# Layer 2 weights as 16-bit exponents with three bf16 parts of the support, in place of the Gelu pair factor of layer 3

## The chip, the cores and the metric

The kernel runs on one core of a Trainium2 chip. The metric is device time in microseconds. Engines are called as in the profile: PE is TensorE, PEld its weight load, DVE VectorE, ACT ScalarE, POOL GpSimd and SP SyncE.

## What is computed

Four graph layers work on N = 3327 nodes with D = 64 features and one sparse weighted adjacency matrix of N x N. Each layer normalises x, cuts it at zero and adds the layer's output to x. Layers 0 (two gated convolutions) and 1 (hyperbolic) are the same in both kernels. The change concerns layers 2 and 3, which are in the reference:

```python
def _L2_gnn_ref(input, adj, weight, bias):
    support = input @ weight
    mask = (adj != 0).astype(support.dtype)
    rank = jnp.cumsum(mask, axis=1)
    deg = rank[:, -1:]
    k = jnp.minimum(deg, float(MAX_NEIGH))
    pos = rank - (deg - k)
    w = mask * jnp.where(pos > 0, DECAY ** (k - pos), 0.0)
    out = w @ support + bias
    return out
...
x_tan = _logmap0(x, C)
left = x_tan @ att_W[:D] + att_b
right = x_tan @ att_W[D:]
adj_att = jax.nn.sigmoid(left + right.T) * adj
x_local = _logmap(x[:, None, :], x[None, :, :], C)
support_t = jnp.einsum('ij,ijd->id', adj_att, x_local)
return _proj(_expmap(x, support_t, C), C)
```

So in layer 2 the weight of a neighbour is a half to the power of the number of neighbours behind it in the row, for at most 100 of them. In layer 3 every pair of nodes has a factor that comes from its hyperbolic distance, and a sigmoid attention, and what is summed over neighbours is that factor, times the attention, times the neighbour's features.

## The kernel before, in words

The nodes are padded to 3328, which makes 26 blocks of 128 (`NB`, `P`). The adjacency comes transposed: one block holds 128 neighbours j on the partitions and all nodes i in the free dimension, 1664 KB. An aggregation keeps the output transposed in four accumulators of PSUM (`acc`); the lower half of their partitions holds the features for the first 1664 nodes (`HN`), the upper half for the others, each in four chunks of 416 (`NQ`, `CH`). The helper of line 241 issues each such matmul; its stationary operand has 64 columns. Four of the 26 adjacency blocks stay resident in SBUF, the rest are streamed anew for each aggregation through three buffers (`adj_block`, L157).

Layer 2 (L349 to L423) goes through the blocks backwards. For each block VectorE makes a 0/1 mask in bf16 (L379). For each of the eight chunks TensorE counts, for each node i, the neighbours behind this one: one matmul with a triangular matrix over the block's mask (L384), which also subtracts 1024 where the mask is set, and one with ones over the sum of the masks of later blocks (`behind`, L392). ScalarE turns the count into the bits of a power of two, as int32 read as f32 (L400). VectorE multiplies it with a test that the count is small enough (L402), and the f32 product `w` goes into the accumulating matmul (L241), two chunks later (`flush(2)`). VectorE adds the mask to `behind` (L416). Here a scheduler chooses the order of instructions on each engine; counts have four banks of PSUM (`scratch`).

Layer 3 is written in an order by hand (`manual_schedule`, L442). The preparation (L487 to L619) packs three bf16 parts of per-node values into rows that DMAs carry into `rows_i`, `rows_j` and `rows_l` (L588, L594). The loop (L743 on) has 26 steps `n`: two output halves times 13 pairs of neighbour blocks. For each, `pair_values` takes one product of 64 features per pair of nodes in f32 (L635) plus a bf16 matmul of the packed rows (L646); ScalarE applies Gelu to the sum (L654), Tanh for the attention (L661), and in two of three steps a Square (L669). VectorE multiplies the attention with the adjacency (L675), in the third of the steps does the square (L680), and multiplies both factors (L687). `gather` sums over neighbours (L703 for the features, L714 for a scalar). A flag `within` (L619) tells whether all squared norms lie in the range for which the fit with Gelu was made. If not, a general version (L763 to L931) recomputes layer 3; on these inputs the branch skips it.

This general version matters below. Its functions are `distances` (L830: per chunk two f32 matmuls, a max with a small number, a second max, then their product), `root_ln` and `root_exp` (L849, L852: ScalarE), `norms` (L855: two VectorE passes), `attention` (L862: Sigmoid, and a product with the adjacency on GpSimd), `logs` (L868: two Ln on ScalarE, a subtraction on GpSimd), `gather` (L875: two products on VectorE, then four matmuls). They work on tiles of 128 x 1664 f32, in groups of two neighbour blocks (`G1 = 2`), in this order:

```python
run(distances, 0)
for g in range(len(groups) + 1):
    ...
    run(root_ln, g)
    run(root_exp, g)
    run(attention, g)
    run(gather, g - 1)
    run(norms, g)
    run(distances, g + 1)
    run(logs, g)
```

The tail (L936 to L982) turns the sums into the output by passes of 128 x 1664 on VectorE.

Of the kernel before, what the change touches and what calls it, by code (L numbers as in the profile page):

```python
# [33 lines left out]
EXP_UNIT = 2.0**23  # L34


X2_LEAST = 22.0
HA = 2.5897813538797263
HB0 = 2.28574309955982
HG = -7.090763495839726  # L40
HK = 0.012618748686465375
HD = 0.7055609776434136 / HK

# [12 lines left out]
def gnn_kernel(ctx: ExitStack, tc: tile.TileContext, t, out):  # L56
# [80 lines left out]
    with ExitStack() as c012:  # L137
# [4 lines left out]
        ps = c012.enter_context(tc.tile_pool(name="ps", bufs=4, space=PSUM))  # L142

        def scratch(name):
            return ps.tile([P, 512], F32, name=name, tag="ps")
# [202 lines left out]

        with ExitStack() as c2:  # L349
# [12 lines left out]
            V.memset(ebias, (127.0 - MASK_ON) * EXP_UNIT)  # L362
# [3 lines left out]
            linear(h_t, w_l2, m_n)  # L366

            acc = accumulators()
            behind = None
            pending = []  # L370

            def flush(keep):
                while len(pending) > keep:
                    accumulate(acc, *pending.pop(0))

            for j in reversed(range(NB)):
                a = adj_block(j)
                mask = mk.tile([P, NP], BF16, name="mask", tag="mask")
                V.tensor_scalar(mask, a, 0.0, None, op0=OP.not_equal)  # L379
                for h in range(2):  # L380
                    for q in range(NQ):
                        i0 = h * HN + q * CH
                        p = scratch("cnt")
                        T.matmul(  # L384
                            p[:, :CH],
                            lhsT=tri,
                            rhs=mask[:, i0 : i0 + CH],
                            start=True,
                            stop=behind is None,
                        )  # L390
                        if behind is not None:
                            T.matmul(  # L392
                                p[:, :CH],
                                lhsT=ones,
                                rhs=behind[:, i0 : i0 + CH],
                                start=False,
                                stop=True,
                            )
                        bits = wk.tile([P, CH], I32, name="bits", tag="bits")
                        S.activation(bits, p[:, :CH], AF.Relu, bias=ebias, scale=-EXP_UNIT)  # L400
                        w = wk.tile([P, CH], F32, name="w", tag="w")
                        V.scalar_tensor_tensor(  # L402
                            w,
                            p[:, :CH],
                            MAX_NEIGH - MASK_ON,
                            bits.bitcast(F32),
                            op0=OP.is_lt,
                            op1=OP.mult,
                        )
                        pending.append((q, h, m_n[:, slot(j), :], w, j == NB - 1, j == 0))  # L410
                        flush(2)
                if behind is None:
                    behind = mask
                elif j:
                    nxt = mk.tile([P, NP], BF16, name="behind", tag="behind")
                    V.tensor_add(nxt, behind, mask)  # L416
                    behind = nxt
            flush(0)
# [14 lines left out]

    c3 = ctx.enter_context(ExitStack())  # L440
    n3 = c3.enter_context(tc.tile_pool(name="n3", bufs=1))
    c3.enter_context(tc.manual_schedule())  # L442

    attw = n3.tile([P, 2, D], F32, name="attw")
    attb = n3.tile([P, 1], F32, name="attb")
    aw, ab = t["att_W"], t["att_b"]
    nc.sync.dma_start(attw, bass.AP(tensor=aw.tensor, offset=aw.offset, ap=[[0, P], [D, 2], [1, D]]))
    nc.sync.dma_start(attb, bass.AP(tensor=ab.tensor, offset=ab.offset, ap=[[0, P], [1, 1]]))
    h = n3.tile([P, NB, D], F32, name="h3")
    sums = n3.tile([P, NB, D + 1], F32, name="sums")  # L450

    with ExitStack() as cf:
        f3 = cf.enter_context(tc.tile_pool(name="f3", bufs=1))
        wk = cf.enter_context(tc.tile_pool(name="wkf", bufs=2))
        ps_acc = cf.enter_context(tc.tile_pool(name="ps_accf", bufs=1, space=PSUM))
        ps = cf.enter_context(tc.tile_pool(name="psf", bufs=1, space=PSUM))

        def pair_tile(i):
            return ps.tile([P, 2, 512], F32, name="pt", tag=("pta", "ptb")[i % 2])


        pairs = [(hf, c) for hf in range(2) for c in range(HB)]
        adj2 = t["adjT"].rearrange("(h c p) n -> c p h n", h=2, p=P)
        adjs = {}

        def load3(n):
            if n < len(pairs):
                hf, c = pairs[n]
                adjs[n] = a = wk.tile([P, 2, HN], F32, name="adj3", tag="adj3")
                nc.sync.dma_start(a, adj2[c][:, :, hf * HN : (hf + 1) * HN])  # L470

        load3(0)
        load3(1)


        rows_j = f3.tile([P, NP], BF16, name="rows_j")
        rows_i = f3.tile([P, NP], BF16, name="rows_i")
        G.memset(rows_j, 0.0)
        G.memset(rows_i, 0.0)
        identb = f3.tile([P, P], BF16, name="identb")  # L480
        V.tensor_copy(identb, ident)
        ones3 = f3.tile([3, P], BF16, name="ones3")
        V.memset(ones3, 1.0)
        hg = f3.tile([P, 1], F32, name="hg")
        V.memset(hg, HG)

        layernorm_relu(n3, h)  # L487

        last = f3.tile([P, 1], I32, name="last")
        G.iota(last, pattern=[[0, 1]], base=0, channel_multiplier=1)  # L490
        lastf = f3.tile([P, 1], F32, name="lastf")
        V.tensor_scalar(lastf, last, P - 1.0, None, op0=OP.is_equal)
        kb = slot(NB - 1)
        V.tensor_scalar(h[:, kb, :], h[:, kb, :], lastf, None, op0=OP.max)
        x2 = sumsq(n3, h, "x2")


        q = small(n3, "q")
        V.tensor_scalar(q, x2, 0.5, -0.5, op0=OP.mult, op1=OP.add)
        V.reciprocal(q, q)  # L500
        xd = f3.tile([P, HB, 3, D], F32, name="xd")
        qv = q.rearrange("p (c a) -> p c a", a=2)
        V.tensor_mul(
            xd[:, :, :2, :],
            h.rearrange("p (c a) d -> p c a d", a=2),
            qv[:, :, :, None].to_broadcast([P, HB, 2, D]),
        )
        G.tensor_copy(xd[:, :, 2, :], xd[:, :, 0, :])

        xs = f3.tile([P, HN], F32, name="xs")  # L510
        xw = f3.tile([P, HN], F32, name="xw")
        for n, (dst, a) in enumerate(((xs, 0), (xw, 1))):
            for c0 in range(0, HB, 8):
                m = min(8, HB - c0)
                p = pair_tile(n + c0 // 8).rearrange("p a b -> p (a b)")
                for c in range(m):
                    T.transpose(
                        p[:, c * P : (c + 1) * P],
                        xd[:, c0 + c, a : a + 2, :].rearrange("p a d -> p (a d)"),
                        ident,  # L520
                    )
                if n:
                    S.activation(dst[:, c0 * P : (c0 + m) * P], p[:, : m * P], AF.Copy)
                else:
                    V.tensor_copy(dst[:, c0 * P : (c0 + m) * P], p[:, : m * P])

        par = f3.tile([P, 4, NB], F32, name="par")
        V.tensor_copy(par[:, 0, :], q)  # L530
        V.tensor_scalar(par[:, 1, :], q, -1.0, -1.0, op0=OP.mult, op1=OP.add)
        V.tensor_scalar(par[:, 2, :], q, -1.0, -HB0 / HA, op0=OP.mult, op1=OP.add)
        pn = small(n3, "pn")
        S.activation(pn, x2, AF.Sqrt)
        V.tensor_scalar(pn, pn, MIN_NORM, None, op0=OP.max)
        kt = artanh(n3, pn, "kt")
        rpn = recip(n3, pn, "rpn")
        V.tensor_mul(kt, kt, rpn)
        sides = []
        for s in range(2):  # L540
            pr = n3.tile([P, NB, D], F32, name="sq", tag="sq")
            V.tensor_mul(pr, h, attw[:, s : s + 1, :].to_broadcast([P, NB, D]))
            r = small(n3, f"side{s}")
            V.tensor_reduce(r, pr, axis=AX.X, op=OP.add)
            V.tensor_mul(r, r, kt)
            sides.append(r)
# [6 lines left out]
        for i in range(3):  # L553
            b = f3.tile([P, 4, NB], BF16, name=f"part{i}")
            V.tensor_copy(b, par)
            if i < 2:
                V.tensor_sub(par, par, b)
# [470 lines left out]
```

## Time and profile before

| | us |
|---|---|
| median of 3 runs | 1162.76 (1161.22 to 1165.96) |
| the profiled execution | 1162.76 |
| its span, from the first to the last instruction | 1160.9 |
| layers 0 and 1 | about 0 to 420 |
| layer 2: preparation, loop | to 470, to 755 |
| layer 3: preparation, loop, tail | to 815, to 1108, to 1161 |

A line of the profile for a group of instructions names the source line, engine, operation, output and inputs by their names in the program, the shape and the count; then follow busy time and the mean duration of one in ns. On the time line the first column is the start and the second the duration, both in us; "x4" means four instructions merged. The time by stretch gives for each stretch its length, then busy us and count of PE, PEld, DVE, ACT and POOL, the clock granted to TensorE, the DMA engines' share and GB/s. The chain of waits follows the last instruction back to what released it. A matmul of f32 shows as two records.

### The profile page before, as it was taken

The page shows a single profiled execution, that of the slowest core. Times are in us where ns is not written, and L with a number is a line of the kernel's source. Part 1 is how long each engine was busy: PE and PEld are TensorE (multiplying, and loading weights), DVE is VectorE, ACT ScalarE, POOL GpSimd, SP SyncE. Part 2 cuts the span into 40 slices and gives each one's busy share as a digit, 9 for nine tenths or more (in the row PEclk, how much of TensorE's full clock was granted, in tenths as well). Part 3 has the DMA queues.
Part 4 walks back from the last instruction along what each step waited for, and adds up shares of the span by engine and source line. Part 5 has one row for each costly group of instructions (what it writes and reads, how often), then busy time and mean ns, then how long its engine had stood idle before and what let it go on. Part 6 is the DMA issues. An engine that isn't in the chain of part 4 may idle for free. (4 is left out here: it accounts for less than half of the span.)

```text
span 1160.9 us, 9585 instructions
## 1 busy us (share of the span) xinstructions
PE 891.9 (77%) x3835; PEld 341.3 (29%) x3835; DVE 638.2 (55%) x716; ACT 386.2 (33%) x452; POOL 9.5 (1%) x18
## 2 busy tenths in 40 slices
PE   2999999997399950999999999911789887889700
PEld 2433453344143320322222222210333333333200
DVE  4000140006800058677777777686588887888778
ACT  1000010002200011444444444400778776787710
POOL 0000000000000000000000000020000000000000
PEclk9999999999599985999999999965899998999955
DMA  8799909993069990143443400020244453444100
GB/s 310 292 385 382 379 5 361 389 396 148 0 255 381 379 385 11 59 176 127 168 164 131 177 1 0 1 120 9 104 147 164 177 177 118 172 145 157 58 3 29
DMA packets 25011, 204.31 MB, mean 176 GB/s; under 512 B 6141, under 2 KB 6269, under 8 KB 13181
## 3 DMA queue, kind: packets, MB, share of 16 engines
q1 hardware_dynamic: 21382, 202.96, 46.0%
q10 hardware_dynamic: 3575, 0.64, 0.3%
q8 instruction: 32, 0.52, 0.2%
q14 instruction: 22, 0.18, 0.0%
HBM read 202.48 MB, written 0.85 MB: 175 GB/s over the span
## 5 line engine op out<-in xcount | busy, mean ns | idle before, releaser
L241 PE MATMUL acc<-adj,m_n 128*64 128x416 f32 x1056 | 271.4, 518 | 15.1 <-DMA adj<-in_adjT 14.7
L241 PE MATMUL acc<-w,m_n 128*64 128x416 f32 x416 | 184.0, 534 | 18.7 <-DVE w L402 18.7
L400 ACT ACTIVATE bits<-cnt,ebias 128x416 int32<-128x416 f32 x208 | 123.2, 606 | 167.2 <-PE cnt L392 156.1
L257 DVE COPY m_t<-acc 128x416 f32<-128x416 f32 x12 | 6.2, 582 | 308.7 <-PE acc L241 308.7
L241 PEld LDWEIGHTS acc<-adj,m_n 128*64 128x64 f32 x1056 | 112.5, 136 | 170.6 <-issue 130.1
L402 DVE SCALAR_TENSOR_TENSOR w<-cnt,bits 128x416 f32<-128x416 f32 x208 | 115.6, 586 | 50.9 <-ACT bits L400 50.7
L675 DVE SCALAR_TENSOR_TENSOR th<-th,adj 128x1664 f32<-128x1664 f32 x52 | 97.5, 1888 | 46.4 <-ACT th L661 46.4
L635 PE MATMUL pt<-xs 64*128 64x416 f32 x208 | 99.2, 558 | 15.4 <-ACT gl L654 15.4
L635 PE MATMUL pt<-xw,xs 64*128 64x416 f32 x208 | 98.8, 556 | 12.3 <-ACT gl L654 12.3
L654 ACT ACTIVATE gl<-pt 128x832 f32<-128x832 f32 x104 | 84.2, 861 | 66.5 <-PE pt L646 66.5
L687 DVE SCALAR_TENSOR_TENSOR gl<-gl,th 128x1664 f32<-128x1664 f32 x52 | 96.0, 1888 | 12.4 <-ACT gl L669 12.1
L703 PE MATMUL accx<-gl,xd 128*64 128x416 f32 x416 | 81.8, 530 | 8.1 <-DVE gl L687 8.1
L280 ACT ACTIVATE gate<-gate,brz 128x416 f32<-128x416 f32 x16 | 9.7, 606 | 234.0 <-PE gate L278 233.9
L661 ACT ACTIVATE th<-leftb,righth 128x1664 f32<-128x1664 f32 x52 | 87.5, 1683 | 0.0
L384 PE MATMUL cnt<-mask,tri 128*128 128x416 bf16 x208 | 71.7, 347 | 1.2 <-DVE mask L379 1.0
L241 PEld LDWEIGHTS acc<-w,m_n 128*64 128x64 f32 x416 | 42.0, 135 | 93.5 <-DVE w L402 46.4
L392 PE MATMUL cnt<-behind,ones 128*128 128x416 bf16 x192 | 65.3, 340 | 0.0
L241 PE MATMUL acc<-res,m_n 128*64 128x416 f32 x192 | 44.0, 545 | 22.2 <-DVE m_n L317 22.2
L416 DVE TENSOR_TENSOR behind<-behind,mask 128x3328 bf16<-128x3328 bf16 x23 | 43.5, 1892 | 30.1 <-PE cnt L392 30.1
L669 ACT ACTIVATE gl<-gl,hg 128x3328 f32<-128x3328 f32 x18 | 55.2, 3069 | 0.0
L197 PE MATMUL tr<-ident,h_n 128*128 128x128 f32 x26 | 5.9, 420 | 63.7 <-DVE h_n L134 63.7
L384 PEld LDWEIGHTS <-tri 128*128 128x128 bf16 x208 | 19.9, 96 | 104.0 <-issue 102.1
(221 smaller groups left out, 713.1 us busy)
## 6 DMA issues: line engine op xcount, KB each, us to landing
adj<-in_adjT SPq DMA_DIRECT2D x114, 1664.0 KB
res<-in_adjT SPq DMA_DIRECT2D x4, 1664.0 KB
xn<-in_x SPq DMA_DIRECT2D x1, 832.0 KB
out<-u SPq DMA_DIRECT2D x1, 832.0 KB
ih<-in_wihT ACTq DMA_DIRECT2D x4, 48.0 KB
hh<-in_whhT ACTq DMA_DIRECT2D x4, 48.0 KB
w<-in_W ACTq DMA_DIRECT2D x4, 16.0 KB
attw<-in_att_W SPq DMA_DIRECT2D x1, 64.0 KB
```

Source lines behind the costliest of these rows:

```text
L241: T.matmul(acc[q][h * D : (h + 1) * D, :CH], lhsT=lhsT, rhs=rhs, start=first, stop=last)
L384: T.matmul(p[:, :CH], lhsT=tri, rhs=mask[:, i0 : i0 + CH], start=True, stop=behind is None,)
L392: T.matmul(p[:, :CH], lhsT=ones, rhs=behind[:, i0 : i0 + CH], start=False, stop=True,)
L400: S.activation(bits, p[:, :CH], AF.Relu, bias=ebias, scale=-EXP_UNIT)
L402: V.scalar_tensor_tensor(w, p[:, :CH], MAX_NEIGH - MASK_ON, bits.bitcast(F32), op0=OP.is_lt, op1=OP.mult,)
L635: T.matmul(pts[b][:, i, :CH], lhsT=xs[rs, c * P : (c + 1) * P], rhs=rhs[rs, q0 : q0 + CH], start=True, stop=False,)
L654: S.activation(gl[:, b, 2 * k * CH : (2 * k + 2) * CH].rearrange("p (i n) -> p i n", i=2), pts[b][:, :, :CH], AF.Gelu, scale=-HA,)
L661: S.activation(th[:, k, :], leftb[:, hf * HN : (hf + 1) * HN], AF.Tanh, bias=righth[:, kk : kk + 1], scale=0.5,)
L669: S.activation(gl, gl, AF.Square, bias=hg)
L675: V.scalar_tensor_tensor(th[:, b, :], th[:, b, :], 1.0, a[:, b, :], op0=OP.add, op1=OP.mult)
L687: V.scalar_tensor_tensor(gl[:, b, :], gl[:, b, :], hd, th[:, b, :], op0=OP.add, op1=OP.mult)
L703: T.matmul(acc[i // 2][(i % 2) * D : (i % 2 + 1) * D, :CH], lhsT=xd[:, c, b, :], rhs=gl[:, b, i * CH : (i + 1) * CH], start=first, stop=last,)
```

## The change

In layer 2 the weights become 16-bit numbers: ScalarE writes the count's power of two straight as the upper 16 bits of a float (`U16`, unit 2**7 instead of 2**23), with a bias that makes counts past the limit zero by the Relu, and the tile is read as bf16. The product on VectorE (L402 of before) is gone. The support, scaled by 2**27, is split into three bf16 parts whose sum is exact, and the accumulating matmuls run once per part in bf16. Counts are in tiles of two banks, two chunks per conversion; the two halves h alternate innermost; the loop is ordered by hand.

In layer 3 the version with Gelu, its preparation, its flag and the branch are gone, and the general version runs always. Its functions are those of before, with small changes ahead of and behind the loop.

```diff
-EXP_UNIT = 2.0**23
+EXP_UNIT = 2.0**7
+U16 = mybir.dt.uint16
...
-            V.memset(ebias, (127.0 - MASK_ON) * EXP_UNIT)
+            V.memset(ebias, (MAX_NEIGH - MASK_ON) * EXP_UNIT)
...
             linear(h_t, w_l2, m_n)
-
+            V.tensor_scalar(m_n, m_n, 2.0**27, None, op0=OP.mult)
+            parts = []
+            for i in range(3):
+                p = mk.tile([P, NB, D], BF16, name=f"part{i}", bufs=1)
+                V.tensor_copy(p, m_n)
+                if i < 2:
+                    V.tensor_sub(m_n, m_n, p)
+                parts.append(p)
...
+            with tc.tile_pool(name="psc", bufs=2, space=PSUM) as psc, tc.manual_schedule():
...
+                def flush(keep):
+                    while len(pending) > keep:
+                        j, k, ws = pending.pop(0)
+                        for i in range(2):
+                            for n, p in enumerate(parts):
+                                for h in range(2):
+                                    accumulate(
+                                        acc,
+                                        2 * k + i,
+                                        h,
+                                        p[:, slot(j), :],
+                                        ws[h][:, i, :].bitcast(BF16),
+                                        j == NB - 1 and n == 0,
+                                        j == 0 and n == 2,
+                                    )
...
+                    V.tensor_scalar(mask, a, 0.0, None, op0=OP.not_equal)
+                    for k in range(NQ // 2):
+                        ws = []
+                        for h in range(2):
+                            p = psc.tile([P, 2, 512], F32, name="cnt", tag="cnt")
+                            for i in range(2):
...
+                            w = wk.tile([P, 2, CH], U16, name="w", tag=f"w{h}")
+                            S.activation(
+                                w, p[:, :, :CH], AF.Relu, bias=ebias, scale=-EXP_UNIT
                             )
-                        bits = wk.tile([P, CH], I32, name="bits", tag="bits")
-                        S.activation(bits, p[:, :CH], AF.Relu, bias=ebias, scale=-EXP_UNIT)
-                        w = wk.tile([P, CH], F32, name="w", tag="w")
-                        V.scalar_tensor_tensor(
-                            w,
-                            p[:, :CH],
-                            MAX_NEIGH - MASK_ON,
-                            bits.bitcast(F32),
-                            op0=OP.is_lt,
-                            op1=OP.mult,
-                        )
-                        pending.append((q, h, m_n[:, slot(j), :], w, j == NB - 1, j == 0))
-                        flush(2)
+                            ws.append(w)
+                        pending.append((j, k, ws))
+                        flush(1)
...
-        for n in range(-1, len(pairs)):
-            if n >= 0:
-                products(n)
-            if n + 1 < len(pairs):
-                pair_values(n + 1)
-                weights(n + 1)
-                load3(n + 3)
...
-        ok = nc.values_load(within, min_val=0, max_val=1)
...
-    with ExitStack() as cg:
-        cg.enter_context(tc.If(ok < 1))
```

The functions of the loop that now runs always, with the line numbers that they have after the change in the first column:

```python
559  p = scratch3(0)
560  T.matmul(p[:, :CH], lhsT=lhsT, rhs=auge[:, cs], start=True, stop=True)
561  V.tensor_scalar(e[:, cs], p[:, :CH], MIN_NORM, None, op0=OP.max)
562  p = scratch3(1)
563  T.matmul(p[:, :CH], lhsT=lhsT, rhs=augd[:, cs], start=True, stop=True)
565  V.scalar_tensor_tensor(d[:, cs], e[:, cs], 2e-7, p[:, :CH], op0=OP.mult, op1=OP.max)
568  V.tensor_mul(e, e, d)
572  S.activation(den[j], den[j], AF.Ln, scale=LN_SCALE)
575  S.activation(den[j], den[j], AF.Exp, scale=-0.5)
579  V.scalar_tensor_tensor(dist[j], dist[j], LN_SCALE**0.5, den[j], op0=OP.mult, op1=OP.mult)
582  V.tensor_scalar(dist[j], dist[j], ONE_LESS, None, op0=OP.min)
587  S.activation(s, leftb, AF.Sigmoid, bias=right[:, k : k + 1])
588  G.tensor_mul(s, s, adjs.pop((hf, j)))
593  S.activation(l, dist[j], AF.Ln, bias=one)
594  S.activation(dist[j], dist[j], AF.Ln, bias=one, scale=-1.0)
595  G.tensor_sub(l, l, dist[j])
599  V.tensor_mul(l, l, den.pop(j))
600  V.tensor_mul(l, l, sig.pop(j))
```

## The prediction

> **What bounds the kernel now.** I read the busy shares first, then the busy time by stretch, and then the time line of one piece of each stretch that the change touches. The stretches are layers 0 and 1 (to 420 us), the preparation of layer 2 (to 470), its loop (to 755), the preparation of layer 3 (to 815), its loop (two stretches, to 1108) and the tail.
>
> ```profile
> span 1160.9 us, 9585 instructions
> ...
> PE 891.9 (77%) x3835; PEld 341.3 (29%) x3835; DVE 638.2 (55%) x716; ACT 386.2 (33%) x452; POOL 9.5 (1%) x18
> ```
> ```profile
> 470.00:755.00 285.00, 264.95 (x833) 68.47 (x833) 201.59 (x261) 122.29 (x207) 0.15 (x1) 1.00 0.28 102
> 755.00:815.00 60.00, 11.35 (x48) 6.64 (x50) 42.43 (x92) 5.04 (x8) 6.57 (x4) 0.59 0.16 62
> 815.00:965.00 150.00, 128.46 (x759) 50.90 (x756) 116.88 (x63) 120.61 (x98) 0.00 (x0) 0.98 0.44 153
> 965.00:1108.00 143.00, 121.86 (x724) 46.93 (x722) 110.89 (x63) 103.46 (x85) 0.00 (x0) 0.97 0.35 127
> ```
>
> The columns are PE, PEld, DVE, ACT and POOL busy, then clock, DMA share and GB/s. In layer 2's loop TensorE is busy 265 of 285 us and the DMA only 28%: TensorE bounds it. In layer 3's loop (293 us) TensorE, VectorE and ScalarE are all at 72 to 86%, and GpSimd is idle. One chunk of layer 2's loop, and one gather of layer 3's, on TensorE:
>
> ```profile
> 504.91 0.35 PE L384 MATMUL cnt<-mask,tri 128*128 128x416 bf16 x1
> 505.10 0.34 PE L392 MATMUL cnt<-behind,ones 128*128 128x416 bf16 x1
> 505.37 0.91 PE L241 MATMUL acc<-w,m_n 128*64 128x416 f32 x2
> 506.21 0.35 PE L384 MATMUL cnt<-mask,tri 128*128 128x416 bf16 x1
> ```
> ```profile
> 904.16 3.01 PE L703 MATMUL accx<-gl,xd 128*64 128x416 f32 x16
> ```
>
> A chunk takes 1.30 us from start to start. A bf16 matmul of 416 columns streams in about 0.175; an f32 one is two records of 0.35 each (416 records for 208 calls). Those sum to 1.05; the other 0.25 goes at the two changes between 128- and 64-column use. In the gather neighbours write alternate halves of the accumulator: 16 records of 0.35 take 3.0 us, so two run side by side.
>
> **What the Trainium skill says.** "TensorE: Matmul & The Clock Gate", Part 3, says that matmuls on different column groups run concurrently; the gather line agrees (0.175 per record instead of 0.35), and layer 2 now does not use it. Its Part 1 says that an idle array falls to half its clock. The trace agrees: layer 3's first f32 passes, after an idle spell, start 0.70 apart (814.21, then 814.90 on the time line), later 0.35. "ScalarE: Activation LUTs", What ACT_TABLE_LOAD costs, gives about 1283 ns per load; the loads in this trace take 1283 ns. "SBUF — State Buffer", Who interferes with whom, says that GpSimd and a VectorE operation that uses two ports, or has two SBUF inputs while GpSimd reads, lock each other out for a whole instruction. For two-port operations the trace agrees:
>
> ```profile
> 757.66 2.95 POOL L479 MEMSET rows_i<- 128x3328 bf16 x1
> ```
> ```profile
> 758.03 2.61 DVE L127 TENSOR_SCALAR ln_mean<-ln_mean 128x26 f32<-128x26 f32 x1
> ```
>
> This small operation takes 0.18 elsewhere and here ends with the memset. For two SBUF inputs no row of before has GpSimd beside it.
>
> **The change, part by part. Layer 2.** It removes 208 f32 products (L402, 586 ns) from VectorE and 416 f32 passes from TensorE. ScalarE has 104 conversions of 832 columns instead of 208 of 416; L654, of that shape, takes 861 ns. For each half block of source nodes (52 of them) TensorE gets 8 count matmuls (8 x 0.175 = 1.40) and 12 bf16 matmuls with neighbours in opposite halves (6 pairs x 0.175 = 1.05), plus one double change of use, 0.25: 2.70 us. Beside it lie ScalarE with 1.7 us, VectorE with 1.9 (mask and running sum, L379 and L416, 3.77 per block), and the DMA with 2.2 per half block at the 390 GB/s of layer 0. The count tile is free in time: its conversion ends some 1 us before TensorE comes back to it, so ordering by hand costs nothing while TensorE is latest; if ScalarE were late by more than that, each half block would grow by the excess.
>
> New ahead of the loop are a scaling and three casts (about 1.0 each, from L379's 1883 ns for twice the elements) and two subtractions (1.9 each): 7.8 us on VectorE, on the path, since the first products need all three parts. They end at 469.6 + 7.8 = 477.4. Two half blocks of counts are done by then, so the end comes at 477.4 + 52 x 2.70 - 1.4 = 616. Now the last product ends at 753. Saved: 137 us, and layer 3 starts at 756 - 137 = 619.
>
> **Layer 3.** Its loop becomes the one that before holds as a fallback (line 763 on) and doesn't run here, so it has to be costed from rows of like shape. Preparation on VectorE, all on the path: normalising 11.2, squared norm 3.9, artanh chain 5.2, three products and two reductions of 1664 elements 9.6, transposed copies (0.85 per 512 columns, as at L202) with their fills 22: 52 us, so it ends at 671. The seven transfers of packed rows (L588, L594) and ScalarE's 21 us of waiting for them go with the old preparation. The loads on SyncE's queue become half as large (0.85 MB) and twice as many; each waits for GpSimd to free one of three buffers, but is wanted a round later, so it is hidden.
>
> A round handles two blocks of neighbours. VectorE: gather, four two-input passes of 1664 elements at 1.9 = 7.65; norms, two of 1.9 and two one-input passes of 1.0 = 5.9; distances, 16 operations of 416 columns from PSUM (0.58 and 0.59 in dependent pairs, 8.9) and two products of 1.9 = 12.7. TensorE needs 16 x 0.70 for the distances and starts them cold after its idle stretch, which I put at 1.3 us. Sum 27.3 us. ScalarE: ten passes of 1.68 and, by the instruction order of the built kernel, three table loads of 1.28: 20.6, and the Exp that the norms need ends 6.3 us into the round, under the gather. GpSimd: four two-input passes. The GPSIMD page's 4497 ns for 2048 elements (GPSIMD Engine Reference, Elementwise) gives an estimate of 3.65 each, 14.6. So VectorE bounds the round: 27.3 without any clash of ports.
>
> The clash is the unknown. Least: none, 27.3. Most: every two-input and two-port pass takes turns with GpSimd: mul after the first norm (9.55 to 13.2), then each following norm pass waits for one GpSimd pass, and the first distance product for the end of the last: 3.65 x 3 + 1.5, a round of 39.9. I take the middle: VectorE's next pass follows 0.02 us after the last one (the chain of waits shows such steps), so I let it keep the port through gather and norms. GpSimd's passes then run during the PSUM operations; each distance product waits for the second of two: 13.55 + 7.3 + 1.9 = 22.75, + 4.45, sub passes to 30.05, + 1.9 = 31.95. If only two-port passes clash, the same count gives 32.4.
>
> A half is: first distances 14, a first round without gather 28.9, eleven rounds of 31.95 = 351.5, and at the end norms, GpSimd's four passes, the last gather and the collection of sums 40.8. That is 435; two of them, with 14 us of transposed copies between, 884. The tail from the last sums now takes 52.4, less 3.9 of waiting at the branch that goes: 48.5. Span: 671 + 884 + 48.5 = 1603.5. The run of the profile was 1162.8 us for a span of 1160.9, and is itself the median of the three; with these 1.9 us: **1605**.
>
> **Rivals.** Taking turns (39.9 per round): a half is 14 + 29.4 + 438 + 44 = 525, so 1786. The skill's sentence on two SBUF inputs speaks for it; against it, the trace never shows GpSimd getting in between two VectorE passes. No clash (27.3): a half is 375, so 1487; against it stands the blocked L127. Layer 2's pairs don't overlap, because each bf16 pass needs its own weight load (135 ns for an f32 one now): 12 x 0.175, or 55 us more, 1660. The other side: not slower needs a round of about 12.5 us (2 x 11 x 12.5, with the other pieces in proportion, fills 1161 - 671 - 48.5 - 14). That could come only if VectorE's f32 two-input passes ran at two elements a cycle; 1.0 us for a one-input pass speaks for such a rate, 1.88 for every two-input row against it, and ScalarE's 20.6 would hold the round anyway. That the change doesn't do what it says, with the fallback already running in before, is excluded: no such line is in its trace.
>
> **Numbers.** Forecast 0.43 (its own range 1570 to 1650); taking turns 0.30; no clash 0.15; pairs apart 0.08; the other side 0.02; the rest, 0.02, lies above. The range reaches over the rivals' times, 1480 to 1800. A measurement of this kernel can tell about 0.5% from no change. Faster 0.02, same 0.01, slower 0.97.
>
> **What would show it.** Layer 2: matmuls of L240 in pairs, 5.4 us per block, a loop of about 140 us with ScalarE at some 60%. Layer 3: 26 rounds, VectorE nearly always busy, ScalarE near 65%, three table loads a round; the duration of L579, L582 and L568 says which clash: 1.9, 1.0 and 1.9 for none, 4 to 6 us where they wait for GpSimd. I am wrong if GpSimd's passes are far from 3.65 us, or if rounds end on ScalarE or TensorE.

## The result, and the profile after

| | us | ratio to before |
|---|---|---|
| before | 1162.28 (beside it) | 1 |
| after, median of 4 runs | 1859.16 (1857.56 to 1864.29) | 1.599, 95% from 1.595 to 1.604 |
| forecast | 1605 (1480 to 1800) | |

The change makes the kernel 697 us slower. The sign was foreseen; the time lies 254 us above the forecast and 59 us above the range. The profiled execution has a span of 1856.7 us. The head of its page, with busy times and the clock granted to TensorE (tenths of full speed, in 40 slices of the span):

```profile
span 1856.7 us, 10430 instructions
...
PE 1231.3 (66%) x3897; PEld 561.0 (30%) x3897; DVE 1245.1 (67%) x1067; ACT 657.1 (35%) x509; POOL 421.2 (23%) x118
...
PEclk9999997995999676556655666675666665566565
```

TensorE is busy for 339 us more than before with only 62 more matmul records, and from the 14th slice on (603 us) its clock is at 0.5 to 0.7 throughout, against 0.97 in layer 3 of before. A matmul takes longer there, so a good part of the added "busy" is the clock and not work. The busy time by stretch (length, then PE, PEld, DVE, ACT, POOL, clock, DMA share, GB/s) puts the time in its place:

```profile
470.00:619.00 149.00, 142.12 (x1039) 68.34 (x1038) 97.39 (x60) 91.80 (x102) 0.00 (x0) 0.98 0.54 199
...
700.00:1232.00 532.00, 334.84 (x587) 145.43 (x586) 437.76 (x311) 243.04 (x160) 196.57 (x49) 0.60 0.12 39
```

Layer 2's loop ends at 615.4 us (forecast 616) with TensorE busy for 95% of it and the clock at 0.98. The stretch from 700 to 1232 us, nearly all of the first half of layer 3's loop, has no engine near its limit: TensorE 63%, VectorE 82% (waits inside its passes included, as shown below), and the clock at 0.60. One half block of layer 2 on TensorE's time line (starts and durations in us):

```profile
540.62 1.25 PE L240 MATMUL acc<-w,part 128*64 128x416 bf16 x12
541.80 0.35 PE L409 MATMUL cnt<-mask,tri 128*128 128x416 bf16 x1
...
543.04 0.34 PE L417 MATMUL cnt<-behind,ones 128*128 128x416 bf16 x1
543.31 1.25 PE L240 MATMUL acc<-w,part 128*64 128x416 bf16 x12
```

From 540.62 to 543.31 is 2.69 us, where the forecast had 2.70. So the search is for layer 3 alone. One round of it on VectorE, from the end of the gather to the first distance:

```profile
1022.61 1.89 DVE L600 TENSOR_TENSOR lnp<-lnp,sig 128x1664 f32<-128x1664 f32 x1
1024.42 1.88 DVE L579 SCALAR_TENSOR_TENSOR dist<-dist,den 128x1664 f32<-128x1664 f32 x1
1026.34 4.42 DVE L582 TENSOR_SCALAR dist<-dist 128x1664 f32<-128x1664 f32 x1
1030.68 5.38 DVE L579 SCALAR_TENSOR_TENSOR dist<-dist,den 128x1664 f32<-128x1664 f32 x1
1036.10 4.39 DVE L582 TENSOR_SCALAR dist<-dist 128x1664 f32<-128x1664 f32 x1
1040.41 0.58 DVE L561 TENSOR_SCALAR den<-pd 128x416 f32<-128x416 f32 x1
```

GpSimd beside it ("x2" is two passes back to back):

```profile
1026.12 8.19 POOL L588 TENSOR_TENSOR sig<-sig,adj 128x1664 f32<-128x1664 f32 x2 [21.92 <-ACT sig L587]
1035.60 4.00 POOL L595 TENSOR_TENSOR lnp<-lnp,dist 128x1664 f32<-128x1664 f32 x1 [1.29 <-ACT dist L594]
1044.06 3.70 POOL L595 TENSOR_TENSOR lnp<-lnp,dist 128x1664 f32<-128x1664 f32 x1 [4.45 <-ACT dist L594]
```

Read the two by their ends. The first L579 is free, 1.88. At 1026.12 GpSimd begins, and the L582 that VectorE issues at 1026.34 lasts until 1030.76, though it needs 1.03. Then L579 (needs 1.88) ends at 1036.06, after GpSimd's second pass (1034.31). The third GpSimd pass is issued at 1035.60 and ends at 1039.60; the last L582 (needs 1.03) ends 0.9 us after it, at 1040.49. VectorE issues its next pass within 0.05 us of the last one, and still a GpSimd pass lies between each two. The lengthened durations are waits; no idle time is shown.

And TensorE in the same round:

```profile
1020.83 7.43 PE L603 MATMUL ac<-lnp,hn 128*65 128x416 f32 x16 [6.33 <-DVE lnp L600]
1028.10 0.86 PE L560 MATMUL pd<-auge,augj 66*128 66x416 f32 x2
...
1030.19 0.86 PE L563 MATMUL pd<-augd,augj 66*128 66x416 f32 x2
1041.04 1.75 PE L560 MATMUL pd<-auge,augj 66*128 66x416 f32 x2 [9.98 <-DVE den L561]
1042.59 1.59 PE L563 MATMUL pd<-augd,augj 66*128 66x416 f32 x2
...
1056.45 1.59 PE L563 MATMUL pd<-augd,augj 66*128 66x416 f32 x2
```

After the gather it runs four distance matmuls ahead, 0.70 us apart, until the four tiles of PSUM for distances are full. Then it idles 9.98 us, while VectorE is in the norms, and the other twelve come 1.39 us apart: half speed, for 17 us, and it never recovers within them. They end the round: in its last block VectorE waits 0.80 us for each.

The round is 43.55 us on VectorE (L599 at 1016.96 and 1060.52): gather 7.46, norms 15.99, distances 20.10.

### The profile page after: what moved, and what is told of

Its sections match the earlier page's. It is cut to its first block, busy times and chain, and to the rows that moved or that the text cites. A ratio compares the mean times of both kernels' runs of the same rounds, so it can differ in the third digit from the quotient of the medians.

```text
span 1856.7 us, 10430 instructions
## 1 busy us (share of the span) xinstructions
PE 1231.3 (66%) x3897; PEld 561.0 (30%) x3897; DVE 1245.1 (67%) x1067; ACT 657.1 (35%) x509; POOL 421.2 (23%) x118
## 4 chain that ended last, share of the span: by engine, by line
PE 30%; issue 26%; DVE 24%; POOL 11%; DMA 8%; ACT 1%; ACTq 0%; POOLq 0%; DVEq 0%
PE acc L240 13%; DMA adj<-in_adjT 7%; POOL lnp L595 6%; POOL sig L588 5%; PE pd L560 5%; PE pd L563 5%; DVE dist L582 5%; DVE dist L579 4%; PE cnt L409 2%; DVE lnp L600 2%; DVE lnp L599 2%; PE cnt L417 2%; DVE den L568 1%; DVE sq L74 1%; PE ac L603 1%
## 5 line engine op out<-in xcount | busy, mean ns | idle before, releaser
L560 PE MATMUL pd<-auge,augj 66*128 66x416 f32 x416 | 289.0, 791 | 235.3 <-DVE den L561 235.2
L588 POOL TENSOR_TENSOR sig<-sig,adj 128x1664 f32<-128x1664 f32 x52 | 212.9, 4114 | 958.2 <-ACT sig L587 958.2
L603 PE MATMUL ac<-lnp,hn 128*65 128x416 f32 x416 | 210.7, 675 | 188.4 <-DVE lnp L600 182.0
L563 PE MATMUL pd<-augd,augj 66*128 66x416 f32 x416 | 284.6, 781 | 0.0
L595 POOL TENSOR_TENSOR lnp<-lnp,dist 128x1664 f32<-128x1664 f32 x52 | 205.6, 3956 | 135.2 <-ACT dist L594 135.2
L572 ACT ACTIVATE den<-den 128x1664 f32<-128x1664 f32 x52 | 82.7, 1590 | 423.7 <-DVE den L568 387.1
L582 DVE TENSOR_SCALAR dist<-dist 128x1664 f32<-128x1664 f32 x52 | 222.3, 4275 | 1.8
L565 DVE SCALAR_TENSOR_TENSOR dist<-den,pd 128x416 f32<-128x416 f32 x208 | 122.3, 588 | 104.6 <-PE pd L563 95.4
L579 DVE SCALAR_TENSOR_TENSOR dist<-dist,den 128x1664 f32<-128x1664 f32 x52 | 182.0, 3500 | 9.1 <-ACT den L575 9.1
L561 DVE TENSOR_SCALAR den<-pd 128x416 f32<-128x416 f32 x208 | 122.1, 587 | 68.8 <-PE pd L560 68.4
L563 PEld LDWEIGHTS pd<-augd,augj 66*128 66x128 f32 x416 | 121.0, 291 | 123.3 <-issue 103.2
L599 DVE TENSOR_TENSOR lnp<-lnp,den 128x1664 f32<-128x1664 f32 x52 | 98.0, 1884 | 7.2 <-POOL lnp L595 7.2
L568 DVE TENSOR_TENSOR den<-den,dist 128x1664 f32<-128x1664 f32 x52 | 98.4, 1891 | 1.8
```

Source lines behind the costliest of these rows:

```text
L560: T.matmul(p[:, :CH], lhsT=lhsT, rhs=auge[:, cs], start=True, stop=True)
L561: V.tensor_scalar(e[:, cs], p[:, :CH], MIN_NORM, None, op0=OP.max)
L563: T.matmul(p[:, :CH], lhsT=lhsT, rhs=augd[:, cs], start=True, stop=True)
L565: V.scalar_tensor_tensor(d[:, cs], e[:, cs], 2e-7, p[:, :CH], op0=OP.mult, op1=OP.max)
L579: V.scalar_tensor_tensor(dist[j], dist[j], LN_SCALE**0.5, den[j], op0=OP.mult, op1=OP.mult)
L582: V.tensor_scalar(dist[j], dist[j], ONE_LESS, None, op0=OP.min)
```

## The experiments

The theory after the result: two things add up. (a) VectorE and GpSimd take turns at each pass; this lengthens the norms by some 10 us. (b) TensorE idles meanwhile, and distance matmuls with 66 rows do not get the clock back. Rivals: (a) alone, with a clock that doesn't matter; (b) alone, with matmuls of 66 rows slow whatever comes before; and layer 2 having a part in it. A round is the distance between the first norm passes of neighbouring rounds, the same for all full rounds of a kernel within the spread given. "One run" is a single execution without an interval. Line numbers differ a little between the kernels.

| kernel | us | full round, us |
|---|---|---|
| after | 1859.2 | 43.5 to 43.6 |
| 128 rows | 1757.9, one run | 39.1 to 39.5 |
| GpSimd's passes on VectorE | 1652.9, one run | 34.0 to 35.8 |
| the same, 128 rows | 1638.1, one run | 34.0 to 35.8 |
| attention late | 1628.5, one run | 32.1 to 33.7 |
| attention late, 128 rows | 1631.4, one run | 32.1 to 33.3 |
| GpSimd's passes left out | 1475.2, one run | 26.6 to 28.5 |

**Layer 2 alone** ("l2only" in what follows). Layer 2 of after with layer 3 of before, the version with Gelu. Against after, only layer 3 is exchanged; the cut shows its first lines:

```diff
-    with ExitStack() as c3:
-        n3 = c3.enter_context(tc.tile_pool(name="n3", bufs=1))
...
+    c3 = ctx.enter_context(ExitStack())
+    n3 = c3.enter_context(tc.tile_pool(name="n3", bufs=1))
...
```

> The new layer 2 with layer 3 left as before (Gelu version). Theory: layer 2's part of the change did what was forecast, a half block of 2.69 us on TensorE instead of four chunks of 1.37, and all of the loss lies in layer 3. Then 1162 - 137 = 1025 us, with layer 3 as long as before. Rival: part of layer 2's gain is only there because layer 3's general version follows it (its loads or its preparation); then over 1040.

Measured: 1028.72 us (1027.24 to 1030.97, 5 runs), ratio 0.885 (0.883 to 0.887). Layer 2's part gains 134 us (1162.3 - 1028.7; forecast 137), and needs no general layer 3 behind it, so the rival falls. What the exchange of layer 3 then adds is 1859.2 - 1028.7 = 830.5 us.

**Layer 2, the two halves h outermost.**

```diff
-                        for i in range(2):
-                            for n, p in enumerate(parts):
-                                for h in range(2):
+                        for h in range(2):
+                            for i in range(2):
+                                for n, p in enumerate(parts):
```

> As l2only, but the twelve accumulating matmuls of a half block run with the half h outermost, so that six neighbours in a row write the same columns of the array. Theory: pairs in opposite column halves stream side by side and halve this step; without them 52 x 6 x 0.175 = 55 us more, about 1080. Rival: the array overlaps them in any order, or ScalarE hides the step: within 10 us of l2only.

Measured: 1050.0 us, one run: 21 us more, between the two. TensorE's time line:

```profile
540.36 1.62 PE L246 MATMUL acc<-w,part 128*64 128x416 bf16 x12
...
543.42 1.62 PE L246 MATMUL acc<-w,part 128*64 128x416 bf16 x12
```

The half block is 3.06 us instead of 2.69. Alternating the halves is worth 0.37 us per twelve products, and the twelve take 1.55 us (the next count starts at 541.91), less than 0.175 each. So the direction was right and the size wrong: the expectation, like the rival of the prediction in which pairs don't overlap, priced it at 55 us. Why six in a row on the same half cost so little is not shown.

**Layer 2, order left to the scheduler.**

```diff
-            with tc.tile_pool(name="psc", bufs=2, space=PSUM) as psc, tc.manual_schedule():
+            with tc.tile_pool(name="psc", bufs=2, space=PSUM) as psc:
```

> As l2only, but the order of layer 2's loop is left to the scheduler; the instruction order shows counts and products of single parts mixed, with two to six products between counts. Theory: more changes between 128- and 64-column use (0.25 us a pair of changes) and fewer opposite neighbours, 20 to 80 us slower than l2only. Rival: the order by hand is worth nothing, within 5 us.

Measured: 1019.6 us, one run; both expectations missed it on the wrong side. The same kernel, run several times:

> Layer 2 as changed but ordered by the scheduler, layer 3 as before, timed in rounds. Theory from its one look: products of the first part start before the other two parts are made, so the loop ends 9 us earlier than by hand: 1019 us, 0.877 of before. Rival: the one look was chance, 1028 us as with the order by hand.

Measured: 1024.35 us (1020.90 to 1027.35, 5 runs), ratio 0.880 (0.878 to 0.883); layer 2 by hand had 0.885 (0.883 to 0.887). The intervals just meet, so these 4 us are likely and not proven by the times. The time lies between the two expectations. The traces show where a gain would come from. TensorE of the version by hand, at the start of the loop:

```profile
469.25 0.37 PE L246 MATMUL acc<-w,part 128*64 128x416 bf16 x2
471.52 0.56 PE L246 MATMUL acc<-w,part 128*64 128x416 bf16 x2 [1.90 <-DVE part L378]
474.51 1.60 PE L246 MATMUL acc<-w,part 128*64 128x416 bf16 x8 [2.43 <-DVE part L378]
```

The written order puts products with all three parts ahead of the next counts, so TensorE waits for VectorE to cast parts 2 and 3. The scheduler uses part 1 and further counts meanwhile. From the start of the first product to that of the last it is 145.1 us by hand (469.2 to 614.4) and 138.2 in both profiles of the scheduled version; the half block is 2.69 us in all. These 7 us are hard to see in the total because the loop itself began at 467.4 us in one of these profiles and at 473.9 in the other. Of the kernels run, this one has the lowest median.

**128 rows.** The operands of the distance products get 62 more rows of zeros (`auge` like `augd`); the results stay the same.

```diff
-        augj = n3.tile([D + 2, NP], F32, name="augj")
+        augj = n3.tile([P, NP], F32, name="augj")
+        G.memset(augj[D:, :], 0.0)
...
-            augd = n3.tile([D + 2, HN], F32, name="augd", tag="augd")
+            augd = n3.tile([P, HN], F32, name="augd", tag="augd")
+            G.memset(augd[D:, :], 0.0)
```

> The changed kernel with the operands of layer 3's distance matmuls padded with zeros from 66 to 128 rows; the result is the same. Theory: after each idle stretch of 10 us the clock stays at half through all 16 matmuls because only 66 of 128 rows are in use; with all rows it recovers as it does for layer 3's matmuls of before, the pitch falls from 1.39 to 0.70 us within a few us, a round loses 5 to 6.5 us and the kernel ends at 1690 to 1730 us. Rival: the number of rows has no part in it, the idle stretch alone keeps the clock low: 1859 us, granted clock of the loop still 0.60.

Measured: 1757.9 us, one run, 101 us less; the theory's range ended 28 us lower, and a round loses 4.4 us instead of 5 to 6.5. The distances after the idle stretch:

```profile
1009.68 1.75 PE L563 MATMUL pd<-auge,augj 128*128 128x416 f32 x2 [8.92 <-DVE den L564]
...
1014.00 1.57 PE L566 MATMUL pd<-augd,augj 128*128 128x416 f32 x2
1015.38 0.88 PE L563 MATMUL pd<-auge,augj 128*128 128x416 f32 x2
1016.10 0.86 PE L566 MATMUL pd<-augd,augj 128*128 128x416 f32 x2
```

Four matmuls come at the slow pace, then the steps fall to 0.70: the clock is back after 5.7 us in this round, and after 3.4 to 5.8 in the others by the trace's record of the granted clock. More zeros to multiply make the kernel faster. The norms are as long as in after (mean 3.50 and 4.28 us), so this round, 39.2 us, is turn-taking with a short cold spell. The rival "taking turns" had predicted 39.9.

**GpSimd's passes on VectorE,** with 66 rows and with 128.

```diff
-                G.tensor_mul(s, s, adjs.pop((hf, j)))
...
-                G.tensor_sub(l, l, dist[j])
...
-                l = lnp.pop(j)
+                l, s = lnp.pop(j), sig.pop(j)
+                V.tensor_mul(s, s, adjs.pop((hf, j)))
+                V.tensor_sub(l, l, dist.pop(j))
                 V.tensor_mul(l, l, den.pop(j))
-                V.tensor_mul(l, l, sig.pop(j))
-                dist.pop(j)
+                V.tensor_mul(l, l, s)
```

> The changed kernel with both GpSimd passes of layer 3's loop (product with the adjacency, difference of logarithms) done by VectorE at the start of the gather. Theory: the norm passes fall from 16.0 to 5.9 us per round since nobody takes turns, the gather grows by four passes of 1.9 to 15.3. The 66-row matmuls still keep the clock at half if the array is idle between the gather's matmuls: round 41.5, about 1805 us; if the shorter idle stretches keep it awake: round 34, about 1610. Rival: the norm passes are slow for a reason of their own (in-place operands, a wait for ScalarE): they stay at 4 to 5 us each, and the kernel gets slower, 2060 us.

> The same with the distance operands padded to 128 rows. Theory: both excesses gone, rounds of 34 to 35.5 us by VectorE alone, 1610 to 1650 us. Rival that the two excesses overlap and cannot both be won: not below 1700.

Measured: 1652.9 and 1638.1 us, one run each. With 66 rows the round is that of the expectation's second case (34), though the time lies 43 us above it; with 128 rows the theory's range holds, and so both rivals fall. VectorE has 4 x 1.9 us more work per round and the kernel is 206 us faster. The norm groups (mean ns after the busy us):

```profile
L579 DVE SCALAR_TENSOR_TENSOR dist<-dist,den 128x1664 f32<-128x1664 f32 x52 | 98.0, 1884 | 9.1 <-ACT den L575 9.1
L582 DVE TENSOR_SCALAR dist<-dist 128x1664 f32<-128x1664 f32 x52 | 53.4, 1027 | 1.8
```

They are back at 1.88 and 1.03. The padding, worth 101 us beside the turns, is worth 15 here. TensorE idles 10.6 us in this kernel too, but ahead of the gather:

```profile
989.27 4.66 PE L602 MATMUL ac<-lnp,hn 128*65 128x416 f32 x8 [10.59 <-DVE lnp L600]
996.72 4.35 PE L602 MATMUL ac<-lnp,hn 128*65 128x416 f32 x8 [2.80 <-DVE lnp L600]
1000.90 0.86 PE L560 MATMUL pd<-auge,augj 66*128 66x416 f32 x2
```

The gather's matmuls have 128 rows, and behind them the distances come 0.70 apart without a pause. So it matters which matmuls follow the pause.

**Attention late.** The Sigmoid and GpSimd's multiply move behind the logarithms, so that GpSimd works beside the distances.

```diff
-                run(attention, g)
                 run(gather, g - 1)
                 run(norms, g)
                 run(distances, g + 1)
                 run(logs, g)
+                run(attention, g)
```

> Same result; in each round of layer 3 the attention step (Sigmoid on ScalarE, then the multiply on GpSimd) is issued after the logs of the round instead of before them, so that GpSimd's four passes fall beside the distances, where VectorE only forms parts and denominators, and not beside the norm passes. One more table load per round. If what costs is GpSimd and VectorE taking turns on passes that TensorE waits for, the norm passes are back at about 1.9 and 1.0 us and the round is 32.5 us, or 33 to 36 with the cold clock: 1590 to 1660 us. Rival: turns cost the same wherever the passes fall in the round, the wait only moves to the denominators, and the time stays near 1859 us (over 1800).

> The same order as in the kernel just before it, with the operands of the distance products padded with zeros from 66 to 128 rows. If the clock that stays at half speed in the distances is the rest of the loss, the round falls to about 32 us and the time to about 1575 us, 20 to 80 us below the kernel with 66 rows. Rival: with the norms free the idle stretch of TensorE is short enough that the clock holds anyway, and the padding changes the time by less than 15 us.

Measured: 1628.5 us, one run, inside the theory's 1590 to 1660; and 1631.4 with 128 rows, one run, where the rival's number, that padding changes nothing, was right, though not its reason (below). Same passes, same engines, one more table load per round: 231 us less by their place in the order. Groups of the first of the two:

```profile
L599 DVE TENSOR_TENSOR lnp<-lnp,den 128x1664 f32<-128x1664 f32 x52 | 175.0, 3365 | 11.4 <-POOL lnp L595 11.4
L568 DVE TENSOR_TENSOR den<-den,dist 128x1664 f32<-128x1664 f32 x52 | 138.4, 2662 | 1.8
```

L579 and L582 are back at 1.88 and 1.03 here too. Turns are still taken: L568 and L599 wait instead, together 2 x (0.77 + 1.48) = 4.5 us per round instead of 10.1. GpSimd's own line says what now sets the round:

```profile
1018.74 9.07 POOL L595 TENSOR_TENSOR lnp<-lnp,dist 128x1664 f32<-128x1664 f32 x2 [15.25 <-ACT dist L594]
1027.77 9.02 POOL L588 TENSOR_TENSOR sig<-sig,adj 128x1664 f32<-128x1664 f32 x2
1052.04 9.07 POOL L595 TENSOR_TENSOR lnp<-lnp,dist 128x1664 f32<-128x1664 f32 x2 [15.25 <-ACT dist L594]
```

The ring of GpSimd's four passes (18.1 us, stretched by VectorE) and 15.25 us from its last product through gather, norms and logarithm to its next input is 33.3 us, the round. A slow spell of the distances hides behind it, hence nothing from padding. The spell is there, and it begins while TensorE works:

```profile
989.94 0.86 PE L563 MATMUL pd<-augd,augj 66*128 66x416 f32 x2
991.49 0.96 PE L560 MATMUL pd<-auge,augj 66*128 66x416 f32 x2 [0.69 <-DVE den L561]
992.29 0.92 PE L563 MATMUL pd<-augd,augj 66*128 66x416 f32 x2
993.00 1.59 PE L560 MATMUL pd<-auge,augj 66*128 66x416 f32 x2
994.39 1.59 PE L563 MATMUL pd<-augd,augj 66*128 66x416 f32 x2
```

Here the pace falls at 993.00, about 10.5 us after the gather, though TensorE has waited only 0.69 us since. With 66 rows the clock falls before the distances are done in 19 of the 22 full rounds. In two of these, the first ones, TensorE waited 3.5 and 3.7 us among the distances; in the other 17 its longest wait was 0.67 to 1.62 us, and in the three rounds without a fall 0.35 to 0.43. With 128 rows, in the same order and with the same waits of up to 1.62 us, the clock fell in none of 20 rounds (and in one of the two first ones). So the number of rows counts for keeping the clock too, and not only for getting it back. With GpSimd's passes on VectorE, where the longest waits among the distances are 0.3 to 0.8 us, 66 rows kept it in all full rounds.

**GpSimd's passes left out.** This kernel leaves out the product of the Sigmoid with the adjacency and the subtraction of the logarithms; the adjacency is still loaded.

```diff
-                G.tensor_mul(s, s, adjs.pop((hf, j)))
+                adjs.pop((hf, j))
...
-                G.tensor_sub(l, l, dist[j])
```

> Leaves out GpSimd's two passes per block of neighbours in layer 3 (the multiply of the Sigmoid by the adjacency block, and the subtraction of the two logarithms; all else stays, the loads of the adjacency too), so the run prices all that these passes cost. Theory (the turns cost some 10 us per round, and the idle stretch that they leave on TensorE is what lets the clock fall in the distances): the round falls from 43.55 us to VectorE's own 26 to 27 and TensorE never waits long enough to be cold throughout: 1859 less 26 rounds of 17, less some 12 us at the end of each half, 1390 to 1440 us. Rival: matmuls of 66 rows hold the clock at half whether or not TensorE idles first; the round is then gather and norms, 13.3, and distances of 20: 33 us, 1560 to 1600 us.

Measured: 1475.2 us, one run, between the theory's total and the rival's. The round decides: 27.3 us, not 33, so the rival falls: the distances with 66 rows run at full speed in all full rounds but the first of the first half, where the clock falls among the last of them. TensorE in the first round, which has no gather, and in a full one:

```profile
693.73 1.76 PE L560 MATMUL pd<-auge,augj 66*128 66x416 f32 x2 [11.22 <-DVE den L561]
695.28 1.59 PE L563 MATMUL pd<-augd,augj 66*128 66x416 f32 x2
...
709.14 1.59 PE L563 MATMUL pd<-augd,augj 66*128 66x416 f32 x2
...
909.27 8.68 PE L602 MATMUL ac<-lnp,hn 128*65 128x416 f32 x16 [6.87 <-DVE lnp L599]
917.79 0.86 PE L560 MATMUL pd<-auge,augj 66*128 66x416 f32 x2
918.49 0.86 PE L563 MATMUL pd<-augd,augj 66*128 66x416 f32 x2
```

In the first round the distances come right after a pause of 11.22 us and stay at 1.39 to the end, with no GpSimd in it: the cold clock comes without any turn-taking. In the full one the gather stands between pause and distances, and they run at 0.70. The theory's total was wrong by my count: of 26 rounds only 22 are full ones, so 22 x 16.3 = 359 us go, not 26 x 17, and the first rounds, cold as shown, are 33.3 us long instead of the 36.7 of after.

## Why the prediction was wrong

**Layer 2: right.** Half block 2.70 forecast, 2.69 measured; end at 616, measured 615.4. The new casts and the two subtractions were on the path of this order, as said; the scheduler's order shows that they need not be.

**Layer 3, the pieces round the loop: nearly right.** First norms at 682.9 us (forecast 671 + 14 = 685). The first rounds of the halves are 36.7 instead of 28.9, the pieces from the last norms of each half on are 7 and 9 us shorter than forecast. Together these come to -2 us; that they cancel is luck.

**The full round: wrong,** 43.55 instead of 31.95. Over 22 rounds that is 255 us, the whole error of the span (1856.7 - 1603.5 = 253). Two steps failed.

First, "so I let it keep the port through gather and norms". It doesn't keep it. A gap of 0.02 us between VectorE's passes means that the next one is issued, not that it has the port; in the round shown, each time a GpSimd pass was waiting, that one came next. The gather was safe only because GpSimd had nothing to do yet (its first input is ready at 1026.1). The price of a turn was right: the estimate of 3.65 us for GpSimd's pass stands against 3.70 measured. Its place and number were not: forecast for gather and norms 13.55 us, measured 23.45; the waits of 4.65 that I put at the two distance products are nil (L568 has a mean of 1.89). The sentence in the Trainium skill, "SBUF — State Buffer", Who interferes with whom, that a VectorE instruction with two SBUF inputs contends with GpSimd's reads, is confirmed by L579 (1.88 alone, 5.38 beside GpSimd), which the trace of before could not show. So the rival "taking turns" had the right mechanism, and with 128 rows its round came nearly true: 39.2 against 39.9.

Second, "starts them cold after its idle stretch, which I put at 1.3 us". I assumed that the clock comes back while the distances run. The Trainium skill, "TensorE: Matmul & The Clock Gate", Part 1, says that it does after some 3.4 us of activity; with 128 rows it took 3.4 to 5.8 us here, with 66 rows it did not come in the 17 us of the round. The distances took 20.1 us against 14.0 in the kernel without GpSimd's passes (27.3 less 13.3 for gather and norms): 6 us more, not 1.3.

The sum of the round's 11.6 us: 9.9 for the turns in the norms, less the 4.65 expected at the distances, and 6.1 for the cold clock (20.1 less the 12.7 + 1.3 forecast). The rest is a slip of addition in the prediction: its own terms 7.65 + 5.9 + 12.7 + 1.3 make 27.55, not 27.3.

The two are coupled. Removing most of the cold spell alone gives 4.4 us per round (43.55 to 39.2); removing the turns, with the passes that cause them, removes both (43.55 to 27.3), because the pause of 9.98 us between the gather and the distances is TensorE waiting for norms that wait for GpSimd.

**The range** ended at the turn-taking rival with its mild cold start. No case held both the turns and the cold clock, because I priced them separately although the turns bring the cold spell on; times above the range had a chance of 0.02.

Two slips of the prediction change nothing here. "Not slower" leaves 1161 - 671 - 48.5 - 14 = 427.5 us for two halves, and with all pieces in proportion that is a round of 31.95 x 213.75 / 435 = 15.7 us, not 12.5. And what starts at 814.90 in the trace of before is a bf16 matmul (L646); the f32 ones at half clock start at 815.25 and 815.94.

**The rest of the loss is the general version itself.** Without any clash, 1475 us is 446 above the kernel with only the new layer 2. VectorE's 27.3 us per pair of blocks and half stand against 293 / 26 = 11.3 in the version with Gelu. The prediction had the size right ("no clash" 1487), in part by luck: its 27.3 holds 1.3 of cold start, which full rounds of that kernel don't have, while the distances take 14.0 at full clock instead of the 12.7 counted on VectorE, because there a matmul comes only every 0.70 us.

## What to carry to other kernels

Before giving GpSimd a pass "for free", put its passes and VectorE's two-input and one-input f32 SBUF passes on one time line and let them alternate; move GpSimd's work beside VectorE passes that read PSUM (0.58 and 0.59 us beside GpSimd and without it here), or do it on VectorE if its own pass (1.9 us here) is shorter than the wait (3.7). When a wait grows on one engine, ask what the pause does to TensorE's clock, and what the first matmuls after it are: matmuls with few rows may leave it at half speed, and may not hold it either. Count full rounds separately from the first and last ones.

## What the hardware showed that I had not expected

- VectorE and GpSimd alternate pass by pass: a one-input pass of 1.03 us took 4.4, a two-input one of 1.88 took 5.4, although VectorE left at most 0.05 us between its passes.
- Matmuls with 66 rows stayed at half speed (1.39 us apart) for 17 us after a pause of 9.98 us; the same products with 62 rows of zeros added sped up to 0.70 after 3.4 to 5.8 us.
- Where 66-row matmuls followed 128-row ones at once, they began at 0.70, but in attention late the clock fell among them 9.5 to 12.7 us after the gather in 17 rounds in which TensorE never waited longer than 1.62 us; with 128 rows and such waits in none of 20. That the number of rows counts is shown; by what measure is not, and no size between 66 and 128 was tried.
- Six bf16 matmuls in a row on the same half of the array's columns, then six on the other, took 1.55 us per twelve against 1.18 when alternated, and not 2.1.
